# Layers: where the Newton steps of the FFN norm's variance stand in VectorE's order

## The chip, the core and the metric

The kernel runs on one core of a Trainium2 chip. A core has five engines that run side by side, each through its own queue of instructions in order: TensorE (PE, matrix products; its weight loads are listed apart as PEld), VectorE (DVE), ScalarE (ACT), GpSimd (POOL) and SyncE (SP, which here only issues DMAs). They meet through semaphores: an instruction that needs another engine's result waits at the head of its queue, and everything behind it waits too.

The metric is the device time of the whole program in microseconds (us), less is better. A profiled execution gives every instruction's start and duration beside it.

## What is computed

An input x of 4 sequences x 512 tokens x 128 channels goes through a pre-norm attention block and then six layers of local attention and a gated FFN:

```python
x = x + attn(layernorm(x))                       # 16 heads of 64, causal penalty
y = layernorm(x)
for i in range(6):
    y = attn_layer(shift_tokens(y), Wqkv[i], q_scale[i], k_scale[i], Wo[i]) + y
    y = ffn_layer(shift_tokens(y), ln_g[i], ln_b[i], W1[i], b1[i], W2[i], b2[i]) + y
x = x + y

def attn_layer(x, Wqkv, qs, ksc, Wo):            # windows of 32 tokens, each sees itself and the one before
    q, k, v = split_heads(x @ Wqkv)
    q, k = l2norm(q) * qs, l2norm(k) * ksc
    q = q * cos * scale + rotate_half(q) * sin * scale
    k = k * cos / scale + rotate_half(k) * sin / scale
    return local_attention(q, k, v) @ Wo

def ffn_layer(x, g, bln, W1, b1, W2, b2):
    mu, var = x.mean(-1), ((x - x.mean(-1)) ** 2).mean(-1)
    xn = (x - mu) / sqrt(var + 1e-5) * g + bln
    a, gate = split(xn @ W1 + b1)
    return a * gelu(gate) @ W2 + b2
```

The change concerns `1 / sqrt(var + 1e-5)` of the FFN's norm.

## The kernel before

The order of every engine's work is written out by hand: the program text is run in order, each operation is put at the end of its engine's queue, and no scheduler moves it. Buffers come from pools of tiles with a fixed number of copies, and waits follow from who wrote or read a tile last.

The first block (to about 575 us) is not touched. The six layers are cut into units: layer i, sequence b, and one of T = 0 to 3 blocks of 128 tokens; 96 units in all, numbered n. The function `slot(n, now, last)` is called once for each n and interleaves the work of several units, so that each engine has something of another unit to do while one waits:

- `u` = unit n: its scores, exponentials and the product with V
- `new` = unit n + 2: its projection to Q, K and V, the rotation and the inverse norms
- `nxt` = unit n + 1: its transposes of Q and K
- `prev` = unit n - 1: its output projection and residual
- `now`: the FFN of a sequence whose attention has just ended, spread over four slots: at T = 0 the token shift, at T = 1 `mean`, at T = 2 `var`, at T = 3 `scale` and the first chunk; `last`, the FFN one sequence before, does chunk 1 at T = 0, chunk 2 at T = 1 and its last product, `out`, at T = 2.

So one slot in four holds a `var`: 24 of them. In such a slot the relevant instructions are, with the lines of the kernel before:

- `var` (L99): TensorE forms the variance as four small products (L102) into PSUM; VectorE adds EPS (L104) into `rs`, 128 x 4 numbers; then `rsqrt` (L74) makes 1 / sqrt from it: two integer operations give a first guess (L79, L80), and three Newton steps of four operations each refine it (L82 to L85). For this norm all 14 run on VectorE. `scale` reads `rs` one slot later (L110, TensorE).
- `rotate(new, 0)` (L477): the rotation of Q. VectorE multiplies the projection, which lies in a PSUM tile, by the two tables (L480 into `rot`, L484 into `t`), 128 x 1024 numbers each. Both read the same PSUM tile, of the group called `two`.
- `add_rotated(new, 0)` (L495): GpSimd adds the two products. `over_norm` (L503), also GpSimd, multiplies by the inverse norms; `carry_k` (L586), GpSimd too, copies the last 32 keys for the next unit.
- `times_v(u, 0)` and `times_v(u, 1)` (L637): TensorE's product with V in two halves. Each takes a PSUM tile of the group `two`; the second half takes the one that `rotate(new, 0)` has read. Behind each half VectorE reads the PSUM tile (L646 reciprocal, L647 product into `on`).
- `last.out()` (L709): the FFN's last product on TensorE, into the `two` tile that the first half of `times_v` has used.

The PSUM group `two` has three tiles, each taken by turn; a tile is taken again only when its last reader is through.

The inverse norms of Q and K (`inverse_norms`, L497) use the same `rsqrt`, there with 128 x 32 numbers, the first two operations on VectorE and the Newton steps on GpSimd.

Of the kernel before, what the change touches and what calls it, by code (L numbers as in the profile page):

```python
# [31 lines left out]
def body(ctx: ExitStack, tc: tile.TileContext, a, out: bass.AP):  # L32
# [5 lines left out]
    nc = tc.nc  # L38
# [3 lines left out]
    NT = S // P  # L42
# [6 lines left out]
    def tmpt(n=S):  # L49
        return tmp.tile([P, n], F32, tag="tmp", name="tmp_t")  # L50
# [23 lines left out]
    def rsqrt(v, n, eng):  # L74

        y = small.tile([P, n], F32, tag=f"y{n}", name="y")
        t = small.tile([P, n], F32, tag=f"yt{n}", name="yt")
        ti = t.bitcast(I32)
        nc.vector.tensor_scalar(ti, v.bitcast(I32), 1, None, ALU.logical_shift_right)  # L79
        nc.vector.tensor_scalar(y.bitcast(I32), ti, -1.0, 1597463007.0, ALU.mult, ALU.add)  # L80
        for k in range(3):
            eng.tensor_tensor(t, y, y, ALU.mult)  # L82
            eng.tensor_tensor(t, t, v, ALU.mult)
            eng.tensor_scalar(t, t, -0.5, 1.5, ALU.mult, ALU.add)
            eng.tensor_tensor(y if k < 2 else v, y, t, ALU.mult)  # L85

    def layernorm_steps(state, bank, inT, outT, g=None, b=None, eng=nc.vector):

        def mean():
            m = bank()
            mm(m, lhsT=avg, rhs=inT(), start=True, stop=True)
            xc = state["xc"] = tmpt()
            nc.vector.tensor_tensor(xc, inT(), m, ALU.subtract)
            sq = state["sq"] = tmpt()
            nc.scalar.activation(sq, xc, AF.Square)

        def var():  # L99
            v = bank()  # L100
            for t in range(NT):
                mm(v[:, t : t + 1], lhsT=state["sq"][:, t * P : (t + 1) * P], rhs=avg[:, 0:1], start=True, stop=True)  # L102
            rs = state["rs"] = small.tile([P, NT], F32, tag="rs", name="rs")
            nc.vector.tensor_scalar(rs, v[:, 0:NT], EPS, None, ALU.add)  # L104
            rsqrt(rs, NT, eng)

        def scale():
            bc = bank()
            for t in range(NT):
                nc.tensor.transpose(  # L110
                    bc[:, t * P : (t + 1) * P], state["rs"][:, t : t + 1].to_broadcast([P, P]), ident
                )
            h = state["h"] = outT()
            nc.vector.tensor_tensor(h, state["xc"], bc, ALU.mult)
            if g is not None:
                nc.vector.tensor_scalar(h, h, g, b, ALU.mult, ALU.add)

        return mean, var, scale

    xT = [None] * B  # L120

# [46 lines left out]
    with tc.manual_schedule():  # L168
# [33 lines left out]
        def norm_x(b):  # L202
            def out_():
                xnT[b] = s1.tile([P, S], F32, tag="xnT", name="xnT", bufs=2)
                return xnT[b]

            return layernorm_steps({}, bank1, lambda: x0T[b], out_, eng=nc.gpsimd if b else nc.vector)
# [30 lines left out]
        class Rows:  # L238


            def __init__(self, b, c, t):
                self.b, self.c, self.t = b, c, t

            def scores(self):
                b, c, t = self.b, self.c, self.t
                sc = self.sc = ps1.tile([P, 2, S], F32, tag="sc", name="ps_sc", bufs=2)
                for k0 in range(0, S, S // 2):
                    for h in range(2):
                        rows = slice(h * HD, (h + 1) * HD)
                        mm(  # L250
                            sc[:, h, k0 : k0 + S // 2],
                            lhsT=qs[b, c][rows, t * P : (t + 1) * P],
                            rhs=ks[b, c][rows, k0 : k0 + S // 2],
                            start=(k0 == 0),
                            stop=False,
                            skip_group_check=True,
                        )
# [84 lines left out]
        mean, var, scale = norm_x(0)  # L342
# [12 lines left out]
        for m in range(last + 1):  # L355
            b, c, odd = m // (2 * NC), m // 2 % NC, m % 2
            now = rows[2 * m : 2 * m + 2]
            old = rows[2 * m - 2 : 2 * m] if m else []
            if m >= 4:
                g = m // 2 - 2  # L360
# [80 lines left out]
    def one_t():  # L441
        return ps_one.tile([P, 512], F32, tag="one", name="ps_one", bufs=2)
# [95 lines left out]
    def new_vw(u):  # L538
        if u.T == 0:
            return vw_first  # L540
        return s2b.tile([P, NW, NC, HD + 1], F32, tag="vw", name="vw", bufs=3)

    def v_windows(u, nxt):


        vt = vts[u.n % 2]
        src = u.p[2].rearrange("p (c a d) -> p a c d", a=2, d=HD)
        for c in range(2):
            nc.scalar.copy(vt[:, c, :, 0:HD], src[:, c])  # L549
        if u.T == 0:  # L550
            u.vw = new_vw(u)
        if nxt is not None:
            nxt.vw = new_vw(nxt)
        for j in range(NW):
            rows = slice(j * W, (j + 1) * W)
            for c in range(2):
                nc.sync.dma_start(out=u.vw[c * HD + W : (c + 1) * HD, j], in_=vt[rows, c])
                if j + 1 < NW:
                    nc.sync.dma_start(out=u.vw[c * HD : c * HD + W, j + 1], in_=vt[rows, c])
                elif nxt is not None:  # L560
                    nc.sync.dma_start(out=nxt.vw[c * HD : c * HD + W, 0], in_=vt[rows, c])
# [113 lines left out]
    class Ffn:  # L675
        def __init__(self, i, b):
            self.i, self.b, self.us, self.st = i, b, [], {}
            self.mean, self.var, self.scale = layernorm_steps(
                self.st,
                one_t,  # L680
                lambda: self.xs,
                lambda: s2.tile([P, S], F32, tag="hT", name="hT", bufs=2),
                vecs[:, i, 0:1],
                vecs[:, i, 1:2],
            )

        def shift(self):
# [50 lines left out]
    def unit(n):  # L738
        return units[n] if 0 <= n < len(units) else None

    def follower(u):
        return units[u.n + 1] if u.T + 1 < NT else None

    def begin(u):

        if u is None or u.T:
            return
        if u.n == 0:
            xs, lt = start
        else:  # L750
            xs = shifted(u.b)
            lt = layer_tables(u.i) if u.b == 0 else units[u.n - 1].lt
        for v in units[u.n : u.n + NT]:
            v.xs, v.lt, v.p = xs, lt, [None] * 3

    def do_project(u, j):
        u.p[j] = project(u, j)
        if u.b + 1 == B and u.T + 1 == NT and u.i + 1 < L:
            wpart[j] = load_part(u.i + 1, j)
# [25 lines left out]
    def slot(n, now, last):  # L785

        u, prev, nxt, new = unit(n), unit(n - 1), unit(n + 1), unit(n + 2)
        T = n % NT  # L790
        part[0] = n % 3
        begin(unit(n + 4))
        if u:
            scores(u)
        if new:
            do_project(new, 0)
            square(new, 0)
        if n == -1:
            y = one_t()
            project_out1(B - 1, y)  # L800
        if u:
            exponents(u)
        if prev:
            project_out_2(prev)
            if prev.b + 1 == B and prev.T + 1 == NT and prev.i + 1 < L:
                wo_w[0] = load_wo(prev.i + 1)
        if new:
            sum_squares(new, 0)
        if prev:
            residual(prev)  # L810
        if now and T > 0:
            (now.mean, now.var, now.scale)[T - 1]()
        if now and T == 0:
            now.shift()
        if new:
            rotate(new, 0)
        if n == -1:
            residual1(B - 1, y)
        if new:
            do_project(new, 2)  # L820
            v_windows(new, follower(new))
        if u:
            transpose_p(u)
        if new:
            add_rotated(new, 0)
            do_project(new, 1)
            square(new, 1)
        if u:
            times_v(u, 0)
        if new:  # L830
            sum_squares(new, 1)
        if nxt:
            transpose_q(nxt)
        if u:
            times_v(u, 1)
        if new:
            inverse_norms(new)
            over_norm(new, 0)
        if nxt:
            transpose_k(nxt)  # L840
        if new:
            rotate(new, 1)
            add_rotated(new, 1)
            over_norm(new, 1)
        if n == -1:
            third_step()
        if nxt:
            carry_k(nxt, follower(nxt))
        if now and T == 3:
            now.chunk(0)  # L850
        if last:
            (lambda: last.chunk(1), lambda: last.chunk(2), last.out)[T]()
        if u:
            transpose_o(u)
# [106 lines left out]
```

## Time and profile before

| | us |
|---|---|
| median of 3 runs | 2291.53 |
| lowest and highest of them | 2286.24 and 2292.44 |
| the profiled execution, its own time | 2288.88 |
| its span, from first to last instruction | 2287.1 |
| TensorE busy in the span | 2193.9 |
| VectorE busy | 1684.3 |
| GpSimd busy | 1453.9 |
| ScalarE busy | 1299.6 |

The granted TensorE clock was 0.996 of full speed. The span is 1.8 us shorter than the execution's own time; the rest lies around it.

How to read the lines further below: a line of a timeline gives start and duration in us, the engine, the line of the kernel, the operation, the tiles it writes and reads (`out<-in`), their shapes (partitions x elements), and in brackets how long the engine had been idle before it and what ended that. A line of the waits' sums gives who waited for whom, the total in us, how often and the longest. A busy engine may be blocked inside an instruction: then the instruction's own duration is longer than its usual one, and no idle time is shown.

### The profile page before, as it was taken

To read this page: it belongs to the slowest core of one execution; us is meant where nothing else is said; L and a number is where in the kernel's file an instruction comes from. 1 tells how busy PE (TensorE), PEld (TensorE's weight loads), DVE (VectorE), ACT (ScalarE), POOL (GpSimd) and SP (SyncE) were. 2 spreads that over 40 slices of the span, in tenths; PEclk is the share of its full clock that TensorE was granted. 3 is DMA by queue.
4 is the path that set the end of the run, shared out by engine and by line. 5 is a ranking of instruction groups with operands and counts; after the bars stand their busy time and mean duration, and the time that the engine had idled before them with its cause. 6 is when DMAs were issued, how large, how long until landed. Compare 5 with 4: busy or idle time off the path is not lost.

```text
span 2287.1 us, 81570 instructions
## 1 busy us (share of the span) xinstructions
PE 2193.9 (96%) x35056; PEld 1445.6 (63%) x35088; DVE 1684.3 (74%) x2608; ACT 1299.6 (57%) x2166; POOL 1453.9 (64%) x1981
## 2 busy tenths in 40 slices
PE   6999999999999999999999999999999999999997
PEld 3555555555566666666666666666666666666664
DVE  3665656655778887788887888878888878888773
ACT  2554545544445666666666656566665666666562
POOL 1544545445777676777676777677766777766760
PEclk9999999999999999999999999999999999999998
DMA  3000000000322233222322323222332223222220
GB/s 117 1 1 1 1 1 1 1 1 1 75 62 68 62 87 74 64 69 68 88 69 61 75 66 94 63 64 68 85 83 61 68 63 87 76 66 71 65 56 15
DMA packets 91025, 125.81 MB, mean 55 GB/s; under 512 B 25262, under 2 KB 39468, under 8 KB 90668
## 3 DMA queue, kind: packets, MB, share of 16 engines
q1 hardware_dynamic: 90236, 119.02, 21.0%
q8 instruction: 279, 4.57, 0.9%
q10 hardware_dynamic: 432, 1.57, 0.2%
q14 instruction: 78, 0.64, 0.1%
HBM read 20.41 MB, written 1.05 MB: 9 GB/s over the span
## 4 chain that ended last, share of the span: by engine, by line
PE 84%; DVE 11%; issue 2%; ACT 1%; DMA 1%; POOL 0%; SPq 0%; POOLq 0%; ACTq 0%; DVEq 0%
PE ps_proj L459 19%; PE ps_one L567 13%; PE ps_one L662 7%; PE ps_att L637 6%; PE ps_att L605 6%; PE ps_sc L250 5%; PE ps_o L321 5%; PE ps_pt L304 4%; PE ps_proj L695 3%; PE ps_proj L696 3%; PE ps_proj L709 2%; DVE t L484 2%; DVE rot L480 2%; DVE yt L79 2%; PE ps_sc L263 2%
## 5 line engine op out<-in xcount | busy, mean ns | idle before, releaser
L495 POOL TENSOR_TENSOR rot<-rot,t 128x1024 f32<-128x1024 f32 x192 | 454.1, 2365 | 197.9 <-DVE t L484 195.3
L459 PE MATMUL ps_proj<-wqkv,xs 128*128 128x512 f32 x1152 | 554.5, 604 | 4.8 <-DVE t L484 3.2
L293 POOL TENSOR_TENSOR pr<-pr,den 128x1024 f32<-128x1024 f32 x128 | 240.8, 1894 | 270.9 <-DVE den L290 269.6
L470 ACT ACTIVATE sq<-ps_proj 128x1024 f32<-128x1024 f32 x192 | 196.9, 1026 | 358.7 <-PE ps_proj L459 305.8
L503 POOL TENSOR_TENSOR rot<-rot,ss 128x1024 f32<-128x1024 f32 x192 | 365.5, 1904 | 14.9
L459 PEld LDWEIGHTS ps_proj<-wqkv,xs 128*128 128x128 f32 x1152 | 198.4, 190 | 167.0 <-issue 146.8
L475 DVE TENSOR_REDUCE ss<-sq 128x16 f32<-128x1024 f32 x192 | 233.2, 1215 | 47.9 <-ACT sq L470 47.2
L275 DVE TENSOR_REDUCE nm<-ps_sc 128x2 f32<-128x1024 f32 x128 | 156.1, 1220 | 122.6 <-PE ps_sc L263 122.6
L480 DVE TENSOR_TENSOR rot<-ps_proj,lt 128x1024 f32<-128x1024 f32 x192 | 233.6, 1217 | 0.0
L484 DVE TENSOR_TENSOR t<-ps_proj,lt 128x1024 f32<-128x1024 f32 x192 | 233.1, 1214 | 0.4 <-POOL rot L495 0.4
L662 PEld LDWEIGHTS ps_one<-aT,wo 128*128 128x128 f32 x1536 | 187.0, 192 | 46.9 <-issue 46.2
L567 PE MATMUL ps_one<-ident,rot 128*128 128x128 f32 x1536 | 210.5, 280 | 4.7 <-issue 2.1
L308 ACT COPY pT<-ps_pt 128x512 f32<-128x512 f32 x128 | 75.1, 587 | 235.4 <-PE ps_pt L304 233.3
L82 POOL TENSOR_TENSOR yt<-y 128x32 f32<-128x32 f32 (+1 forms) x309 | 73.5, 238 | 209.6 <-DVE y L80 193.3
L615 DVE TENSOR_REDUCE mx<-ps_att 128x16 f32<-128x1024 f32 x96 | 117.5, 1224 | 101.6 <-PE ps_att L605 99.9
L662 PE MATMUL ps_one<-aT,wo 128*128 128x128 f32 x1536 | 187.9, 275 | 1.2 <-issue 0.9
L281 ACT ACTIVATE pr<-ps_sc,nm 128x512 f32<-128x512 f32 x256 | 175.1, 696 | 9.7 <-DVE nm L275 9.7
L567 PEld LDWEIGHTS ps_one<-ident,rot 128*128 128x128 f32 x1536 | 164.5, 141 | 24.0 <-issue 4.4
L637 PEld LDWEIGHTS ps_att<-vw,pT 64*32 64x32 f32 x9216 | 103.2, 105 | 93.2 <-ACT pT L570 53.7
L549 ACT COPY vt<-ps_proj 128x512 f32<-128x512 f32 x192 | 103.2, 590 | 93.9 <-PE ps_proj L459 92.3
L304 PEld LDWEIGHTS ps_pt<-ident,pr 128*128 128x128 f32 x1024 | 118.6, 142 | 55.9 <-issue 47.4
L637 PE MATMUL ps_att<-vw,pT 64*32 64x65 f32 x9216 | 128.9, 225 | 24.1 <-DVE t L484 14.5
(132 smaller groups left out, 3996.1 us busy)
## 6 DMA issues: line engine op xcount, KB each, us to landing
vw<-vt SPq DMA_DIRECT2D x1152, 65.0 KB, 2.1
vw_first<-vt SPq DMA_DIRECT2D x336, 65.0 KB, 2.0
wqkv<-in_wqkv_dram SPq DMA_DIRECT2D x18, 512.0 KB, 7.3
wo<-in_wo_dram SPq DMA_DIRECT2D x6, 512.0 KB
w<-in_w_dram SPq DMA_DIRECT2D x6, 341.0 KB, 4.0
xr<-in_x_dram SPq DMA_DIRECT2D x4, 256.0 KB, 5.6
out_dram<-tmp_t SPq DMA_DIRECT2D x4, 256.0 KB
w<-in_w_dram SPq DMA_DIRECT2D x12, 64.0 KB, 2.9
```

The source lines that it names most:

```text
L293: nc.gpsimd.tensor_tensor(self.pr, self.pr, self.den.unsqueeze(2).to_broadcast([P, 2, S]), ALU.mult)
L304: nc.tensor.transpose(pt[:, k * P : (k + 1) * P], self.pr[:, h, k * P : (k + 1) * P], ident)
L459: mm(p[:, c, :], lhsT=u.xs[:, u.T * P : (u.T + 1) * P], rhs=wpart[j][:, c * 512 : (c + 1) * 512], start=True, stop=True,)
L470: nc.scalar.activation(u.sq, u.p[j], AF.Square)
L475: nc.vector.tensor_reduce(u.ss[:, j * HEADS : (j + 1) * HEADS], heads(u.sq), AX.X, ALU.add)
L480: nc.vector.tensor_tensor(heads(t0), heads(pf), lt[:, u.T, 2 * j].unsqueeze(1).to_broadcast([P, HEADS, HD]), ALU.mult)
L484: nc.vector.tensor_tensor(t1.rearrange("p (h t d) -> p h t d", t=2, d=half), pf.rearrange("p (h t d) -> p h t d", t=2, d=half)[:, :, ::-1, :],
L495: nc.gpsimd.tensor_tensor(u.r[j], u.r[j], u.t1, ALU.add)
L503: nc.gpsimd.tensor_tensor(heads(u.r[j]), heads(u.r[j]), u.ss[:, j * HEADS : (j + 1) * HEADS].unsqueeze(2).to_broadcast([P, HEADS, HD]), AL ...
L567: nc.tensor.transpose(tp[:, c * P : (c + 1) * P], src[:, (4 * g + c) * P : (4 * g + c + 1) * P], ident)
L637: mm(o[j * W : (j + 1) * W, h, c * (HD + 1) : (c + 1) * (HD + 1)], lhsT=u.pT[h * HD : (h + 1) * HD, 4 * g + c, j * W : (j + 1) * W], rhs=u ...
L662: mm(y[:, 0:P], lhsT=wo_w[0][:, c, :], rhs=u.aT[:, c, :], start=(c == 0), stop=(c == NC - 1))
```

## The change

`layernorm_steps` can hand out the Newton part as a step of its own, `roots`. The FFN's norm asks for that, and `slot` calls it, in the slot with T = 2, behind `rotate(new, 0)`, the projection of V and the copies of V's windows. The other norms keep it inside `var`.

```diff
-    def layernorm_steps(state, bank, inT, outT, g=None, b=None, eng=nc.vector):
+    def layernorm_steps(state, bank, inT, outT, g=None, b=None, eng=nc.vector, apart=False):
...
             rs = state["rs"] = small.tile([P, NT], F32, tag="rs", name="rs")
             nc.vector.tensor_scalar(rs, v[:, 0:NT], EPS, None, ALU.add)
-            rsqrt(rs, NT, eng)
+            if not apart:
+                roots()
+
+        def roots():
+            rsqrt(state["rs"], NT, eng)
...
-        return mean, var, scale
+        return (mean, var, scale, roots) if apart else (mean, var, scale)
...
     class Ffn:
...
-            self.mean, self.var, self.scale = layernorm_steps(
+            self.mean, self.var, self.scale, self.roots = layernorm_steps(
...
                 vecs[:, i, 1:2],
+                apart=True,
             )
...
         if new:
             do_project(new, 2)
             v_windows(new, follower(new))
+        if now and T == 2:
+            now.roots()
         if u:
             transpose_p(u)
```

In VectorE's order the 14 operations of `rsqrt` stand between L104 and L480 before the change, and between L484 and L646 after it. In the last two of the 24 slots there is no `new`, and VectorE's order is the same as before. The orders of the other engines do not change. Lines named in the text are those of the kernel before; in the changed kernel L104 has become L105, those from L107 to L685 have moved down by 5, those behind by 6, and those behind the new call by 8.

## The prediction

> **What bounds the kernel now.** I read the busy row and the chain on the page first, then the sums of waits, then the timeline of the slots that the change touches, engine by engine.
>
> ```profile
> PE 2193.9 (96%) x35056; PEld 1445.6 (63%) x35088; DVE 1684.3 (74%) x2608; ACT 1299.6 (57%) x2166; POOL 1453.9 (64%) x1981
> PE 84%; DVE 11%; issue 2%; ACT 1%; DMA 1%; POOL 0%; SPq 0%; POOLq 0%; ACTq 0%; DVEq 0%
> ```
>
> TensorE is busy for 96% of the span, so only its idle time can be won: 2287.1 - 2193.9 = 93 us in all. The sums of waits say how much of that hangs on Q's and K's rotation (line 484, the second of its two VectorE products):
>
> ```profile
> PE ps_att L637 <- DVE t L484: 14.5, 21, 1.7
> PE ps_proj L459 <- DVE t L484: 3.2, 6, 0.7
> ```
>
> The first line is the stall in question: the second half of the product with V (L637) waits for the PSUM bank that the rotation of Q still reads. (The columns are total us, times, longest.) Its longest is 1.7 us, in the first of the affected slots (L104 at 696.32 us); the other 20 add up to 12.8 us, 0.17 to 0.88 us each, and one further slot has next to none. In the timeline every one of them lies in the slot in which `var` runs (T = 2); in the other three kinds of slot TensorE's bubbles are mostly its own issue. A typical one on VectorE, then TensorE and GpSimd:
>
> ```profile
> 1251.70 0.16 DVE L104 TENSOR_SCALAR rs<-ps_one 128x4 f32<-128x4 f32 x1
> 1251.90 1.63 DVE L79 TENSOR_SCALAR yt<-rs 128x4 int32<-128x4 int32 x1
> 1253.56 0.31 DVE L80 TENSOR_SCALAR y<-yt 128x4 int32<-128x4 int32 x1
> 1253.90 0.16 DVE L82 TENSOR_TENSOR yt<-y 128x4 f32<-128x4 f32 x1
> ...
> 1256.09 0.16 DVE L85 TENSOR_TENSOR rs<-y,yt 128x4 f32<-128x4 f32 x1
> 1256.17 1.22 DVE L480 TENSOR_TENSOR rot<-ps_proj,lt 128x1024 f32<-128x1024 f32 x1
> 1257.30 1.22 DVE L484 TENSOR_TENSOR t<-ps_proj,lt 128x1024 f32<-128x1024 f32 x1
> 1258.43 0.20 DVE L646 RECIPROCAL rden<-ps_att 128x8 f32<-128x8 f32 x1
> 1258.66 0.69 DVE L647 TENSOR_TENSOR on<-ps_att,rden 128x512 f32<-128x512 f32 x1
> ```
> ```profile
> 1258.57 0.86 PE L637 MATMUL ps_att<-vw,pT 64*32 64x65 f32 x64 [0.68 <-DVE t L484]
> 1259.36 1.09 PE L567 MATMUL ps_one<-ident,rot 128*128 128x128 f32 x8
> 1260.29 2.74 PE L709 MATMUL ps_proj<-tmp_t,w 128*128 128x512 f32 x6
> ```
> ```profile
> 1251.60 1.90 POOL L503 TENSOR_TENSOR rot<-rot,ss 128x1024 f32<-128x1024 f32 x1
> 1253.45 0.40 POOL L586 COPY kT<-kT 128x256 f32<-128x256 f32 x1
> 1258.60 2.37 POOL L495 TENSOR_TENSOR rot<-rot,t 128x1024 f32<-128x1024 f32 x1 [4.75 <-DVE t L484]
> ```
>
> From here on every time is counted from the start of L104 in its slot (1251.70 here). L79 takes 1.63 us and not its usual 0.17: it ends at 0.20 + 1.63 = 1.83, just behind GpSimd's L503 (end 1.80); L80 ends with the copy L586. The rotation therefore starts at 4.47 and ends at 6.82, and L637 follows at 6.87.
>
> [...] L79 ran 1.01 to 1.86 us in 21 of the 22 slots that the change touches, while L480 and L484 (one input in PSUM) stay at 1206 to 1225 ns everywhere. [...] Here 128x4 operations take 161 to 170 ns and start every 0.20 us. [...]
>
> **The change, part by part.** It touches 22 of the 24 slots with `var`; in the last two there is no new unit, so nothing stands between. No instruction is added or removed and no DMA moves. On VectorE 14 small operations (L79, L80 and three times L82 to L85) go behind L480 and L484. TensorE's, ScalarE's, GpSimd's and SyncE's orders stay.
>
> (1) Rotation earlier. L480 needs the projection, ready since about 1248.9, and can start 0.08 before L104's end as it does now behind L85: at 0.10. Its pair takes 2.35, so L484 ends at 2.44 instead of 6.82. L637's second half is ready at 6.87 - 0.68 = 6.19 and waits no longer. Gain: the whole 12.8 us, and 1.7 us in the first slot.
>
> (2) The Newton chain meets another GpSimd instruction. The addition L495 starts 0.08 after L484's end (1258.60 against 1258.52), with the copy L586 out of the way by 1.5 to 2.5: at 2.52. L79 starts 0.09 before L484's end, as L646 does now, and is through at 2.52; L80 comes 0.03 later[...]. The same meeting is in the trace once, with L503 in L495's place:
>
> ```profile
> 834.09 0.17 DVE L79 TENSOR_SCALAR yt<-rs 128x4 int32<-128x4 int32 x1
> 834.29 1.78 DVE L80 TENSOR_SCALAR y<-yt 128x4 int32<-128x4 int32 x1
> ```
> ```profile
> 834.15 1.90 POOL L503 TENSOR_TENSOR rot<-rot,ss 128x1024 f32<-128x1024 f32 x1
> ```
>
> So L80 ends at 2.52 + 2.37 + 0.04 = 4.93. The other twelve take 2.35 (1253.90 to 1256.25) from 4.96: the chain ends at 7.31. GpSimd has nothing more to start until VectorE's next inverse norm, so there is no second meeting.
>
> (3) What stands behind it. Next in VectorE's queue is L646, at 7.23 instead of 6.73, and L647 ends at 8.15 instead of 7.65. L647 empties the bank that L709, the FFN's last product, writes. Without the old stall TensorE reaches L709 at 8.59 - 0.68 = 7.91; it must now wait until 8.15 + 0.06 = 8.21. New stall about 0.29 in 21 slots: 6 us. The first slot has no L709; there L647 of the second half holds the transposes about as long as today, so I count no gain in it.
>
> (4) Everything else lies under cover. `rs` is next read one slot later (L110, at 17.6). VectorE's later work in the slot (L475, second rotation, L711) slides by 0.5 and still ends at 13.55, before the scores that its maximum waits for (13.7); it idles 0.9 to 1.4 us there now, so a further 0.2 is free, and beyond that the exponentials still have over 1 us. GpSimd's inverse-norm chain also starts 0.5 later. In the next slot L116 waits for its L503, and the rotation of Q there ends 0.5 later while TensorE comes 0.4 earlier; the slack between that rotation and L637 is 1.26 to 1.7 us in those slots today, so some 0.4 remains.
>
> Sum: 12.8 - 6 = 6.8 us gained, taken from the profiled run's 2288.88 (span 2287.1 and 1.8 around it): 2282.1. The profiled run is 2.65 under the median of the three runs, and the four executions average 2289.8; 2289.8 - 6.8 = 2283. I take 2283.
>
> **Bounds of the unknown costs.** The order of L79 and L495 has never been seen. If L79 itself is caught, the chain ends 0.2 later, the stall is 0.49 and the gain 12.8 - 10.3 = 2.5. If nothing is caught, the chain ends at 2.35 + 14 x 0.20 = 5.15, which is when L637's first half is through (start 1256.01, 0.86 long: 5.17): L709 never waits and the gain is 14.5 at most, the first slot's included. I take the middle because three meetings in the trace (696, 834 and 2227 us) all let one operation in flight pass and catch the next.
>
> **Rivals.**
> - No meeting: GpSimd yields to the small operations. For it: they follow each other with gaps of only 0.03. Against it: the three meetings named. 2289.8 - 14.5 = 2275.
> - Given back whole: the chain ends 0.3 later than I say (L79 caught, and slower restarts), so that L709 waits as long as L637 did. For it: 0.2 comes from one step. Against it: it takes two slips at once. About 2289.
> - Slower: GpSimd's addition is itself late, because the copy L586 waits for ScalarE's kT copies. If L586 ends at 3.6, as it does in the first slot, L495 runs from 3.66 to 6.03, the chain ends at 8.45 and L709 starts at 9.35. Today it starts at 7.91 + 12.8 / 21 = 8.52 on average, so 21 slots cost 0.83 each, 17 us: 2307. It decides from an L495 start of about 2.85 on, where the new stall equals the old 0.61. Against it: in the other 21 slots L586 ends by 2.5.
>
> **How the numbers follow.** My forecast 0.66, no meeting 0.13, given back 0.12, slower 0.09. About 0.3% (6.9 us) is what a measurement of this kernel can tell from no change. My forecast's own range, 2.5 to 9.5 us gained, (its top is a chain 0.13 shorter) straddles that: 0.40 faster, 0.25 same, 0.01 slower. No meeting is faster (0.13), given back 0.02 faster and 0.10 same, the last slower. Together 0.55, 0.35, 0.10. The range 2275 to 2290 takes in both ends of the meeting and leaves out the slower case and the scatter at the edges.
>
> **What would show it.** Right: L80 of the 128x4 chain near 2.4 us in most of the 22 slots, L79 back at 0.17, L637's wait for L484 gone, and a new wait of L709 for L647 of about 0.3 us, 21 times. Wrong: L80 short (then more is gained), L79 long, or waits of L637 for L484 in the slots after (then the slack in (4) was too small).

## The result and the profile after

| | before | after |
|---|---|---|
| median, us | 2289.87 (22 runs) | 2292.84 (22 runs) |
| lowest to highest, us | 2285.14 to 2293.34 | 2288.82 to 2299.47 |
| profiled execution, its span, us | 2288.88, 2287.1 | 2289.91, 2288.1 |

The ratio is 1.0014 with a 95% interval of 1.0008 to 1.0021: the changed kernel is slower by 3 us, where 7 us less were forecast. In the changed kernel L480 has become L485, L484 L489, L495 L500, L637 L642, L646 L651, L647 L652, L605 (the score products) L610, L567 (the transposes) L572 and L709 L715.

The busy row of the page of after:

```profile
PE 2194.7 (96%) x35056; PEld 1444.1 (63%) x35088; DVE 1701.6 (74%) x2608; ACT 1298.8 (57%) x2166; POOL 1451.1 (63%) x1981
```

TensorE's busy time is the same to 0.8 us, and so is its idle time. VectorE has gained 17 us of "busy" time without a new instruction. By their durations, which overlap their neighbours' a little, L79 and L80 of this chain take 13.7 us more in all, and L116 (L121 in the changed kernel), the FFN norm's last scaling in the slot behind, takes 7.0 more. The timeline of after shows the first of these, in the slot that was shown of before, VectorE first, then GpSimd, then TensorE:

```profile
1251.88 0.16 DVE L105 TENSOR_SCALAR rs<-ps_one 128x4 f32<-128x4 f32 x1
1251.96 1.21 DVE L485 TENSOR_TENSOR rot<-ps_proj,lt 128x1024 f32<-128x1024 f32 x1
1253.09 1.22 DVE L489 TENSOR_TENSOR t<-ps_proj,lt 128x1024 f32<-128x1024 f32 x1
1254.22 0.16 DVE L79 TENSOR_SCALAR yt<-rs 128x4 int32<-128x4 int32 x1
1254.42 2.35 DVE L80 TENSOR_SCALAR y<-yt 128x4 int32<-128x4 int32 x1
...
1258.99 0.16 DVE L85 TENSOR_TENSOR rs<-y,yt 128x4 f32<-128x4 f32 x1
1259.07 0.20 DVE L651 RECIPROCAL rden<-ps_att 128x8 f32<-128x8 f32 x1
1259.30 0.69 DVE L652 TENSOR_TENSOR on<-ps_att,rden 128x512 f32<-128x512 f32 x1
...
1261.27 0.69 DVE L652 TENSOR_TENSOR on<-ps_att,rden 128x512 f32<-128x512 f32 x1
```
```profile
1254.39 2.35 POOL L500 TENSOR_TENSOR rot<-rot,t 128x1024 f32<-128x1024 f32 x1 [0.66 <-DVE yt L79]
```
```profile
1258.01 0.86 PE L642 MATMUL ps_att<-vw,pT 64*32 64x65 f32 x64
1258.80 1.09 PE L572 MATMUL ps_one<-ident,rot 128*128 128x128 f32 x8
1260.05 2.84 PE L715 MATMUL ps_proj<-tmp_t,w 128*128 128x512 f32 x6 [0.16 <-DVE on L652]
```

L79 got through, L80 started 0.03 us after GpSimd's addition (L500) and ended 0.03 after it. The second half of the product with V (L642, 1258.01) no longer waits; L715 waits for L652. Inside the slot that is the forecast almost to the digit. What the forecast does not have is in the sums of waits (total us, times, longest) over 690 to 2147 us, the stretch of the 84 slots from the first changed one to the last. After:

```profile
PE ps_att L642 <- issue: 12.5, 16, 1.3
PE ps_att L610 <- issue: 7.1, 14, 1.7
PEld ps_proj L715 <- DVE on L652: 6.7, 17, 0.4
PE ps_one L572 <- DVE ss L504: 1.3, 1, 1.3
```

and the same rows of before, where the first kind of wait is the one that the change removes:

```profile
PE ps_att L637 <- DVE t L484: 13.6, 20, 1.7
PE ps_att L637 <- issue: 7.3, 10, 1.3
PE ps_att L605 <- issue: 3.3, 8, 0.6
```

"issue" means that no semaphore explains the wait. The trace's DMA records explain it. The page has a row for them (queue and kind, packets, MB, share of the DMA engines' time):

```profile
q8 instruction: 279, 4.57, 0.9%
```

Each of these packets is of 16 KB (4.57 MB in 279), and the trace has 71,555 TensorE instructions (35,056 matmuls, 35,088 weight loads and 1,411 that are neither): one packet for about every 256. Each of the 38 such waits of after, and of the 25 of before, between 690 and 2200 us (those over 0.1 us; the rows above count from 0.15) ended 2.2 to 3.1 us after the start of the latest packet, which itself took 0.9 to 1.7 us. And all 63 fall on one place of a count by 256: with all of TensorE's instructions numbered in order, the one that waits always stands at place 161 or 162 of its 256, as is to be expected if it or its weight load is the first of an awaited packet. From these two counts I take the packets for TensorE's instructions: it was waiting for its own. These waits, with a few that bear another name but end in the same way, are called fetch waits below. Most stand where TensorE uses up instructions fastest: in the scores (128 products in 1.6 us, each with a weight load) and in the product with V (64 in 0.86 us). Packets are numbered from 0 in the order of their start.

Put together by kind of slot (T), from the slots' starts and the waits in each, 84 slots:

| | T=0 | T=1 | T=2 | T=3 | all | fetch waits T=2, T=3, all |
|---|---|---|---|---|---|---|
| before, us | 348.6 | 361.6 | 389.9 | 357.0 | 1457.1 | 1.2, 8.6, 14.6 |
| after, us | 350.4 | 361.3 | 386.7 | 363.1 | 1461.5 | 4.3, 14.8, 25.5 |

The changed slots themselves (T = 2) gained 3.2 us; the slots behind them (T = 3), in which nothing was changed, lost 6.1, as much as their fetch waits grew (6.2).

### The profile page after: what moved, and what is told of

Same layout as the page of the kernel before. It is cut to its first block, busy times and chain, and to the rows that moved or that the text cites. A ratio compares the mean times of both kernels' runs of the same rounds, so it can differ in the third digit from the quotient of the medians.

```text
span 2288.1 us, 81570 instructions
## 1 busy us (share of the span) xinstructions
PE 2194.7 (96%) x35056; PEld 1444.1 (63%) x35088; DVE 1701.6 (74%) x2608; ACT 1298.8 (57%) x2166; POOL 1451.1 (63%) x1981
## 3 DMA queue, kind: packets, MB, share of 16 engines
q8 instruction: 279, 4.57, 0.9%
## 4 chain that ended last, share of the span: by engine, by line
PE 84%; DVE 11%; issue 2%; ACT 1%; DMA 1%; POOL 0%; SPq 0%; POOLq 0%; DVEq 0%; ACTq 0%
PE ps_proj L464 19%; PE ps_one L572 13%; PE ps_one L667 7%; PE ps_att L610 6%; PE ps_att L642 5%; PE ps_sc L255 5%; PE ps_o L326 5%; PE ps_pt L309 4%; PE ps_proj L701 3%; PE ps_proj L702 3%; PE ps_proj L715 3%; DVE y L80 2%; PE ps_sc L268 2%; DVE t L489 1%; DVE rot L485 1%
## 5 line engine op out<-in xcount | busy, mean ns | idle before, releaser
L500 POOL TENSOR_TENSOR rot<-rot,t 128x1024 f32<-128x1024 f32 x192 | 453.4, 2362 | 100.6 <-DVE t L489 59.7
L480 DVE TENSOR_REDUCE ss<-sq 128x16 f32<-128x1024 f32 x192 | 233.1, 1214 | 47.9 <-ACT sq L475 47.5
L485 DVE TENSOR_TENSOR rot<-ps_proj,lt 128x1024 f32<-128x1024 f32 x192 | 233.6, 1217 | 0.0
L489 DVE TENSOR_TENSOR t<-ps_proj,lt 128x1024 f32<-128x1024 f32 x192 | 233.3, 1215 | 0.4 <-POOL rot L500 0.4
L572 PE MATMUL ps_one<-ident,rot 128*128 128x128 f32 x1536 | 210.4, 280 | 5.6 <-POOL rot L500 2.5
L572 PEld LDWEIGHTS ps_one<-ident,rot 128*128 128x128 f32 x1536 | 164.5, 141 | 25.0 <-issue 4.7
L642 PEld LDWEIGHTS ps_att<-vw,pT 64*32 64x32 f32 x9216 | 103.1, 105 | 81.8 <-ACT pT L575 54.0
L642 PE MATMUL ps_att<-vw,pT 64*32 64x65 f32 x9216 | 129.1, 225 | 13.8 <-issue 13.3
```

What stands on the lines that cost most here:

```text
L480: nc.vector.tensor_reduce(u.ss[:, j * HEADS : (j + 1) * HEADS], heads(u.sq), AX.X, ALU.add)
L485: nc.vector.tensor_tensor(heads(t0), heads(pf), lt[:, u.T, 2 * j].unsqueeze(1).to_broadcast([P, HEADS, HD]), ALU.mult)
L489: nc.vector.tensor_tensor(t1.rearrange("p (h t d) -> p h t d", t=2, d=half), pf.rearrange("p (h t d) -> p h t d", t=2, d=half)[:, :, ::-1, :],
L500: nc.gpsimd.tensor_tensor(u.r[j], u.r[j], u.t1, ALU.add)
L572: nc.tensor.transpose(tp[:, c * P : (c + 1) * P], src[:, (4 * g + c) * P : (4 * g + c + 1) * P], ident)
L642: mm(o[j * W : (j + 1) * W, h, c * (HD + 1) : (c + 1) * (HD + 1)], lhsT=u.pT[h * HD : (h + 1) * HD, 4 * g + c, j * W : (j + 1) * W], rhs=u ...
```

## The experiments

Each is compared with the kernel before on the same chip. Slot sums and fetch waits come from one profile each. At the start two theories stood against each other: S, that the loss lies in VectorE's and GpSimd's lag behind the changed place, and F, that TensorE's fetch is a second bound just under the waits, so that no removal of waits could gain.

**e1_mid: the chain between the two products of the rotation.**

```diff
-    def rotate(u, j):
+    def rotate(u, j, between=None):
...                                       # L480 is here
+        if between:
+            between()
         t1 = u.t1 = s2a.tile([P, INNER], F32, tag="t1", name="t1", bufs=3)
...                                       # L484 is here
-            rotate(new, 0)
+            rotate(new, 0, now.roots if now and T == 2 else None)
...
-        if now and T == 2:
+        if now and T == 2 and not new:
             now.roots()
```

> The 14 Newton operations stand between the two products of Q's rotation. They then start before GpSimd's addition can, end at about 4.6 us after L104, the rotation ends at 5.8 and frees its PSUM tile before TensorE's product with V asks for it (6.1), and the reciprocal comes at 5.7 instead of 7.2, so the FFN's last product need not wait either. Both theories expect the 12.8 us of waits of before and the 6 us of waits of after to be gone from the T = 2 slots. Theory S (what was lost lies in VectorE's and GpSimd's lag behind the change): the time falls by the whole, 12 to 15 us against before (ratio 0.9935 to 0.9948). Theory F (TensorE's fetch of its own instructions is a second bound just under the waits): the waits named issue rise from 12.8 us (before, from 690 to 2147 us) to over 22, and the time is within 5 us of before (ratio 0.998 to 1.002).

Measured: 2276.83 against 2287.46 us, ratio 0.9955 (0.9943 to 0.9968). Its VectorE in a T = 2 slot:

```profile
766.34 0.16 DVE L105 TENSOR_SCALAR rs<-ps_one 128x4 f32<-128x4 f32 x1
766.42 1.22 DVE L485 TENSOR_TENSOR rot<-ps_proj,lt 128x1024 f32<-128x1024 f32 x1
767.55 0.68 DVE L79 TENSOR_SCALAR yt<-rs 128x4 int32<-128x4 int32 x1
768.27 0.30 DVE L80 TENSOR_SCALAR y<-yt 128x4 int32<-128x4 int32 x1
...
770.88 1.22 DVE L491 TENSOR_TENSOR t<-ps_proj,lt 128x1024 f32<-128x1024 f32 x1
772.01 0.20 DVE L653 RECIPROCAL rden<-ps_att 128x8 f32<-128x8 f32 x1
```

GpSimd's addition cannot start before L491 is through, so the chain only meets the end of an older operation (L79: 0.68). The reciprocal comes 5.67 after L105 instead of 7.19, and the FFN's last product starts at 7.84 without waiting, which gives the place from which after's wait is counted: 8.17 - 7.84 = 0.33 us. F falls in its strong form: 10.6 us are to be had. S had asked for 12 to 15, so its number was missed too. The slots with T = 3 took 358.6 us, not 363.1.

**e2_no_newton: the chain left out.**

```diff
-            nc.vector.tensor_scalar(rs, v[:, 0:NT], EPS, None, ALU.add)
-            rsqrt(rs, NT, eng)
+            if g is None:                 # the other norms, as before
+                nc.vector.tensor_scalar(rs, v[:, 0:NT], EPS, None, ALU.add)
+                rsqrt(rs, NT, eng)
+            else:
+                nc.vector.tensor_scalar(rs, v[:, 0:NT], 0.0, 0.02, ALU.mult, ALU.add)
```

> Left out: the FFN norm's inverse root; rs is set to a constant 0.02 in the place of L104, so the 14 small operations of 24 slots are gone and the result is not the reference's. Nothing stands in the rotation's way and nothing behind it is delayed: this is the ceiling of any place for these operations. Theory S: 13 to 17 us less than before (ratio 0.9925 to 0.9943). Theory F: at most 5 us less (ratio 0.998 or more), with the waits named issue at over 22 us.

Measured: 2273.35 against 2287.46, ratio 0.994 (0.9928 to 0.9953): 14 us, which S had and F had not. The waits named issue came to 22.6 us, 10 more than before; that half of F held, so part of what is freed can go into fetch. The 84 slots took 1448.3 us, no less than in e1_mid (1445.8): between the two products the chain costs the slots nothing that this run can show.

**e3_before_fill128 and e4_after_fill128: other packet borders.** 64 small products at the start of TensorE's queue shift every packet border by 128 instructions of the count by 256.

```diff
+        fill = bank1()
+        for k_ in range(64):
+            mm(fill[0:32, (k_ % 8) * 64 : (k_ % 8 + 1) * 64], lhsT=avg[0:HD, 0:W], rhs=avg[0:HD, 0:HD], start=True, stop=True)
         rows = [Rows(b, c, t) for ...]
```

> The kernel before with 64 small products into an unread PSUM tile at the start of TensorE's queue, where it waits for the first input until 5.4 us: 128 more TensorE instructions, half of what one instruction packet of 16 KB holds, and nothing else. They are done before 5.4 us. Theory S: the time does not change (ratio 0.999 to 1.001). Theory F: the packets' borders fall on other instructions, so the waits named issue stand in other slots and their sum changes by several us either way; the time follows it, up to 0.4% either way.

> The changed kernel with the same 128 TensorE instructions at its start. Theory S: as the changed kernel, ratio 1.0005 to 1.0025 against before. Theory F: the sum of the waits named issue differs from the 22.2 us of the changed kernel, and the time with it; against e3_before_fill128 it can be faster or slower, by less than the 6.8 us that the sum of waits alone promised.

Measured: 2292.52 (ratio 1.0022, 1.0015 to 1.003) and 2296.51 (1.0044, 1.0031 to 1.0056). The fill was not free as I had expected: it took 13.9 us where 4.3 were idle, and the layers began 6 us later in both (597.1 and 597.3 us instead of 591.1 and 591.4). So the whole times say nothing about the borders. The 84 slots do: 1457.3 us against 1457.1 without the fill, and 1459.1 against 1461.5. The waits named issue came to 15.7 us in e3 and 23.9 in e4 (12.8 and 22.2 without the fill). The changed kernel is behind with either placing of the borders, by 1.8 us with the fill and by 4.4 without it: where they fall decides part of the size.

**e5_hold: the change's order, but without the meeting.** A small GpSimd copy that reads `rs` stands in front of the addition, so GpSimd waits for the chain. Theory M says that the meeting of L80 with the addition (2.35 us in after) turns the change's gain into a loss.

```diff
         if new:
+            if now and T == 2:
+                held = small.tile([P, NT], F32, tag="held", name="held")
+                nc.gpsimd.tensor_copy(held, now.st["rs"])
             add_rotated(new, 0)
```

> The changed kernel, with one small GpSimd copy of rs in front of the addition of Q's products in the T = 2 slots: GpSimd's addition then starts only when the Newton chain is through[...]. The chain should end at 5.2 us after L104 instead of 7.3, the second operation (L80) take 0.2 to 0.3 us instead of 2.35, and the FFN's last product start at 7.84 without a wait. Theory M[...]: the time is that of e1_mid, ratio 0.994 to 0.997 against before. Theory S (the change's order itself is bad, the lag behind it costs): ratio 0.999 or more.

Measured: 2276.19 against 2287.09, ratio 0.9958 (0.9943 to 0.9973). VectorE and GpSimd in a T = 2 slot of it (L105 at 764.11):

```profile
766.45 0.16 DVE L79 TENSOR_SCALAR yt<-rs 128x4 int32<-128x4 int32 x1
766.65 0.17 DVE L80 TENSOR_SCALAR y<-yt 128x4 int32<-128x4 int32 x1
...
769.45 0.21 DVE L651 RECIPROCAL rden<-ps_att 128x8 f32<-128x8 f32 x1 [0.24 <-PE ps_att L642]
```
```profile
769.27 0.19 POOL L835 COPY held<-rs 128x4 f32<-128x4 f32 x1 [3.55 <-DVE rs L85]
769.41 2.37 POOL L500 TENSOR_TENSOR rot<-rot,t 128x1024 f32<-128x1024 f32 x1
```

L80 is back at 0.17 us, and the loss of 3 us has become a gain of 11. The order that the change makes is not the fault; the meeting of L80 with GpSimd's addition is, with 2.2 us on VectorE per slot. GpSimd's addition starts 2.8 us later than in after, and the time is that of e1_mid all the same. The waits named issue were 20.3 us, 4.5 more than in e1_mid, but not in the slots with T = 3 (9.1 us): their sum alone does not tell what a kernel loses.

**e6_mid_late_on and its control e9_mid_late_rot.** What is left is how a delay on VectorE that TensorE does not visibly wait for costs time in the next slot. Theory Q says that a late `on` makes TensorE's next packet of instructions late. Both take e1_mid and add one reduction of 1.14 us in the T = 2 slots: e6 in front of the second half of `on`, e9 behind it.

```diff
# e6: in front of sum_squares(new, 1); e9: in front of inverse_norms(new)
+            if now and T == 2:
+                extra = small.tile([P, HEADS], F32, tag="extra", name="extra")
+                nc.vector.tensor_reduce(extra, tabs.rearrange("p t f d -> p (t f) d"), AX.X, ALU.add)
```

> e1_mid with one more VectorE reduction (128x1024, 1.14 us, result unread) between the first and the second half's reading of the product with V, T = 2 slots only. The second half of `on` then comes about 1.85 us after the start of the FFN's last product, as in the changed kernel (1.9), instead of 0.7; TensorE asks for it 2.6 us after that start, so TensorE itself waits for nothing more. Theory Q[...]: the packets at the end of the T = 2 slots (54, 75, 128, 202, 223) start 0.5 to 1 us later against the next slot's scores than in e1_mid, waits named issue stand in those scores, 2 to 4 us in all, and the time is 2 to 4 us over e1_mid. Without that mechanism: the time of e1_mid within 1 us.

> The control to e6_mid_late_on: the same extra VectorE reduction (1.14 us) in the same slots, but behind the second half of `on` and in front of the inverse norms. The second rotation, GpSimd's Newton chain and everything after them come as late as in e6_mid_late_on; only `on` comes as early as in e1_mid. Theory Q[...]: the packets at the end of the T = 2 slots stand where e1_mid has them (1.3 to 1.7 us ahead of the next scores), no waits named issue in those scores, and the time is within 2 us of e1_mid, ratio 0.995 to 0.9965 against before. Theory S (the lag of VectorE and GpSimd in the slots behind is what costs): as e6_mid_late_on, ratio 0.997 to 0.9985.

Measured: e6 2281.07 against 2287.09 (0.9977, 0.9969 to 0.9985); e9 2277.73 against 2286.77 (0.9956, 0.9942 to 0.997). The packets that come at the end of a T = 2 slot, by how long before the next slot's scores (the band products at their start) they began, in us (negative: behind that start):

| packet | before | after | e1_mid | e6_mid_late_on | e9_mid_late_rot |
|---|---|---|---|---|---|
| 54 | 0.96 | 0.14 | 1.31 | 0.65 | 1.61 |
| 75 | 0.70 | 0.41 | 1.61 | 0.25 | 1.54 |
| 128 | 0.83 | 0.27 | 1.63 | 0.30 | 1.17 |
| 202 | 0.84 | -0.44 | 1.39 | 0.50 | 1.31 |
| 223 | 1.12 | 0.38 | 1.61 | -0.39 | 1.43 |

In all 25 cases the packet began 1.2 to 2.2 us after the second half of `on` was through, wherever that stood: 2.5 to 2.6 us ahead of the scores in before, 1.7 in after, 2.8 to 3.2 in e1_mid, 1.5 to 2.1 in e6, 2.9 to 3.2 in e9.

TensorE around packet 75, in after, e1_mid and e6_mid_late_on:

```profile
913.31 2.84 PE L715 MATMUL ps_proj<-tmp_t,w 128*128 128x512 f32 x6 [0.17 <-DVE on L652]
916.00 1.04 PE L572 MATMUL ps_one<-ident,on 128*128 128x128 f32 x8
916.96 0.41 PE L599 MATMUL ps_att<-band,ident 64*32 64x512 bf16 x8
917.19 1.29 PE L610 MATMUL ps_att<-kT,qT 64*32 64x64 f32 x108
919.33 0.41 PE L610 MATMUL ps_att<-kT,qT 64*32 64x64 f32 x20 [0.85 <-issue]
```
```profile
913.81 1.04 PE L574 MATMUL ps_one<-ident,on 128*128 128x128 f32 x8
914.77 0.41 PE L601 MATMUL ps_att<-band,ident 64*32 64x512 bf16 x8
915.00 1.54 PE L612 MATMUL ps_att<-kT,qT 64*32 64x64 f32 x128
```
```profile
914.17 1.04 PE L574 MATMUL ps_one<-ident,on 128*128 128x128 f32 x8
915.14 0.41 PE L601 MATMUL ps_att<-band,ident 64*32 64x512 bf16 x8
915.36 1.29 PE L612 MATMUL ps_att<-kT,qT 64*32 64x64 f32 x108
917.22 0.41 PE L612 MATMUL ps_att<-kT,qT 64*32 64x64 f32 x20 [0.56 <-issue]
```

and the scores of before at this place, and the second half of `on` in the same order, after, e1_mid, e6:

```profile
916.53 1.76 PE L605 MATMUL ps_att<-kT,qT 64*32 64x64 f32 x128
```
```profile
914.53 0.69 DVE L652 TENSOR_TENSOR on<-ps_att,rden 128x512 f32<-128x512 f32 x1
```
```profile
911.24 0.69 DVE L654 TENSOR_TENSOR on<-ps_att,rden 128x512 f32<-128x512 f32 x1
```
```profile
912.94 0.69 DVE L654 TENSOR_TENSOR on<-ps_att,rden 128x512 f32<-128x512 f32 x1
```

In none of the three does the transpose of `on` (L572, L574) wait. Yet with `on` late the packet starts late (at 916.55 in after, 0.41 us ahead of the scores, and at 914.89 in e6, 0.25 ahead; at 913.17 in e1_mid, 1.61 ahead), and in after and e6 the scores stop behind the same product, the 108th. In e1_mid and before they run through. The sums of the scores' waits over 690 to 2147 us, e1_mid, e6 and e9:

```profile
PE ps_att L612 <- issue: 4.4, 8, 2.0
```
```profile
PE ps_att L612 <- issue: 7.0, 15, 1.0
```
```profile
PE ps_att L612 <- issue: 1.7, 5, 0.5
```

(2.0 of e1_mid's 4.4 are one wait at packet 43, behind the first changed slot; e6 and e9 have none there.) The T = 3 slots took 358.6, 361.6 and 357.7 us, their fetch waits 9.4, 13.1 and 8.2. Clearest are those of them that stand at a packet from the end of a T = 2 slot (the five of the table, and 96, 149, 170 and 244): 3.8 us in e6 and 3.6 in after, none in e1_mid, e5_hold and e9, and 0.2 in before. All 84 slots took 1445.8, 1451.5 and 1444.9 us, with 15.8, 22.8 and 15.2 us of waits named issue. The same 1.14 us of VectorE work brings T = 3 more fetch waits when it delays `on`, and none behind `on`, although everything later on VectorE and GpSimd is then equally late (the inverse norms start 9.58 us after L105 in e6 and 9.57 in e9, 8.45 in e1_mid; medians). In these slots S falls, and a late `on` is shown to make the fetch late. The longer L121 falls as a cause with it: its 24 runs take 37.2 us in e9 and 37.6 in after. Against the whole times that were expected, e6 lost more than 2 to 4 us: 0.0022 of the ratio, 5 us.

**e7_before_again, e8_after_again: chance or kernel.** Both kernels once more, unchanged, one run each.

> The kernel before, a second profile. If the fetch waits depend on the kernel and not on the run: the waits named issue between 690 and 2147 us come to 10 to 16 us, with none at packets 54, 75, 128 and 223 nor in the product with V of the T = 2 slots with packets 42, 95, 169 and 243. If they are chance: they stand elsewhere and the sum is 9 to 22 us.

> The changed kernel, a second profile. If the fetch waits depend on the kernel: the waits named issue come to 19 to 25 us, with those at packets 42, 95, 169 and 243 (0.5 to 1 us each) and at 54, 75, 128 and 223 there again. If they are chance: elsewhere, sum 9 to 22 us.

Measured: 2286.29 us for before and 2296.83 for after. The waits named issue came to 14.7 us in before and 22.2 in after (first profiles 12.8 and 22.2), the T = 3 slots to 357.5 and 364.2, the 84 slots to 1457.6 and 1461.6. The sums belong to the kernel. Single packets scatter: in before, 54, 95 and 169 now had waits of 0.18, 0.20 and 0.71 us, and in after packet 128 had none and packet 95 only 0.40, both against what I had expected.

**e10_mid_again: the yardstick.**

> e1_mid once more, on the same chip as e9_mid_late_rot, as its yardstick: ratio 0.9943 to 0.9968 against before, the waits named issue between 690 and 2147 us at 14 to 18 us and the T = 3 slots at 358 to 359 us in all, if its fetch waits depend on the kernel and not on the run.

Measured: 2271.07 against 2286.77, ratio 0.9934 (0.992 to 0.9947); issue 15.4 us; 84 slots 1443.5, T = 3 357.3. Ratio and T = 3 are a little lower than was expected. On the same chip e9 is 6.7 us slower, not within 2. Of the 6.8 us between the two profiled runs 1.4 lie in the 84 slots, 2.9 ahead of them and 2.6 behind, where the edit changes next to nothing; that part is unexplained and stays open. e1_mid and e10_mid_again (one kernel, 0.9955 and 0.9934) and e5_hold (0.9958) are the two orders that beat both kernels.

## Why the prediction was wrong

**What held.** The order of events in the changed slot, by its own steps, from L105's start: rotation through at 2.43 (2.44 said), GpSimd's addition at 2.51 (2.52), L80 2.35 us long in 21 of 22 slots (about 2.4), chain through at 7.27 (7.31), L646 at 7.19 (7.23), the FFN's last product at 8.17 (8.21), its delay 0.33 (0.29). Two small slips: 0.16 - 0.08 puts the rotation's start at 0.08, not 0.10, and TensorE is ready for the FFN's last product at 7.84 (e1_mid), not 7.91. The first slot gained nothing, as was said: its 1.7 us came back as a wait of 1.3 for VectorE and 0.7 of fetch. What the meeting of L80 with the addition costs inside the slot was right, and e5 shows that the meeting decides.

**What failed: step (4), "everything else lies under cover".** It weighs every delay on VectorE and GpSimd by one question, whether the engine that reads the result comes later still, and puts what passes at nothing; the second half of `on`, which comes later too, it does not list. By that question `on` passes, for its transposes do not wait. But the packet at the end of the slot comes 1.2 to 2.2 us behind `on`: with `on` through 1.7 us ahead of the next slot's scores and not 2.5, the packet starts later (0.41 us ahead of the scores and not 0.70 at packet 75), and the scores, which use 256 instructions in some 1.6 us, stop (0.85 us there). Against the two profiles of before, the T = 3 slots of the two of after lost 6.4 us (363.7 against 357.2); their fetch waits grew by 5.6. Of these 3.4 stand at packets that came behind a late `on`; e1_mid and e5_hold, where `on` comes early, have none of them. Another 1.7 stand at packet 43, behind the first changed slot, and do not hang on a late `on`: e1_mid, e2_no_newton and e5_hold have that wait too (1.4 to 2.0 us). I had read every engine's queue and not the DMA queue of instructions (q8, 279 packets); the row for it was on the page, and "issue" in the sums of waits, and I took both as given.

**A part of step (1) failed too**: "the whole 12.8 us". In four T = 2 slots (packets 42, 95, 169, 243) the wait for L484 had covered a fetch wait at the same product; with it gone 0.67, 0.94, 0.67 and 1.03 us of fetch came out in the first profile of after; over all T = 2 slots the two profiles have on average 2.8 us more than those of before. e1_mid has these too (2.4 us), so they belong to any removal of that wait. So, it seems, does the wait at packet 43, which was not followed further.

**The sum, mended**, over the 84 slots, means of two profiles each: waits for L484 -13.9 in T = 2 and -0.7 in T = 1; the FFN's last product 17 x 0.33 = +5.6; the first slot's new wait +1.3; fetch waits from 15.1 to 24.3, +9.2. Together +1.5 us; measured +4.2 (1461.6 against 1457.4), so 2.7 us stay unassigned. Of the 20 such products in these slots 17 were held up; in the other three (packets 95, 169, 243) a fetch wait just before had delayed TensorE already. The forecast had the waits for L484 in T = 2 and the FFN's last product, 6.8 us gained in all. From there to the 4.2 lost it is 11.0 us, and the fetch waits are 9.2 of them: 3.4 from step (4), 2.8 in T = 2 and the 1.7 at packet 43 from the removal of the wait, the rest scattered.

The case "given back whole" named nearly the right time (2289) for a wrong reason, a longer chain, so it was near by luck, and the slower case's mechanism, a late copy L586, did not occur outside the first slot.

How a late `on` makes the packet late was not shown. The runs show the two ends of it, `on` and the packet 1.2 to 2.2 us behind it, not what lies between.

## What to carry to other kernels

Moving small VectorE work behind a large operation was not free here: GpSimd's addition started at that moment, and L80 took 2.35 us, where it takes 0.17 in e5_hold. So look at what the large operation releases on GpSimd, and place the small work before that release (e1_mid) or make GpSimd wait for it (e5_hold). On an engine that is busy nearly all the time, waits named "issue" deserve a look of their own: where instructions are short, a wait that is removed can uncover one for instructions (0.67 to 1.03 us in four slots here), and an operand that comes later but still in time can bring one about in the next stage (0.85 us at packet 75). A sum of removed waits is a ceiling until those are looked at.

## What the runs showed of the hardware

- TensorE's fetch waits, read as waits for its own instructions: 15 us in before, 24 in after. The 63 over 0.1 us that are named issue in the two first profiles ended 2.2 to 3.1 us after a 16 KB packet's start, each at place 161 or 162 of a count by 256 of its instructions.
- Where the chain meets GpSimd's addition in after, the operation in flight passed and the next was held until 0.03 us behind the addition's end, 21 times out of 22: L79 0.16 us, then L80 2.35. VectorE's gap of 0.03 us between the two was enough for GpSimd to come in: its addition starts 0.01 us behind L79's end and 0.03 ahead of L80.
- A 1.14 us delay of an operand that no engine waits for moved an instruction packet by 0.7 to 2.0 us (e6 against e1_mid); the same work behind that operand moved it by 0.5 at most (e9).
